# Gate, context and transposed-context transfers moved along the queue of an attention pipeline, and one group's modulation by another engine

## The chip, the cores and the metric

The program runs on one core of one Trainium2 chip. The metric is the device time of one execution in microseconds (us). Before the change it is 1631.61 us, the median of three runs (1629.51 to 1631.78). "PE" is TensorE, "DVE" VectorE, "ACT" ScalarE, "POOL" GpSimd and "SP" SyncE, which here computes nothing: it issues transfers (DMAs).

## The reference

128 sequences of 64 tokens with 128 channels pass through four layers. What matters here is the attention: 16 heads of 8 channels, in float32.

```python
# L0 (a DiT block): mod = silu(cond) @ adaln_w + adaln_b, cut in six
xm = ln(x) * (1 + sc_sa) + sh_sa
x = x + g_sa * (attend(xm @ qkv_w + qkv_b) @ sa_proj_w + sa_proj_b)      # "L0s", self
x = x + attend(ln(x) @ q_w, ctx @ kv_w) @ ca_proj_w + ca_proj_b          # "L0c", cross
x = x + g_ff * mlp(ln(x) * (1 + sc_ff) + sh_ff)
# L1: cross attention with modulated norms of x and ctx                     "L1c"
# L2: as L0, with ln(ctx) in the cross part                                 "L2s", "L2c", MLP
# L3: 1-head attention over ctx, router, three experts, a gate
```

attend is softmax(q k^T / sqrt(8)) v for each head; the sum of the weights is divided out behind the product with v.

## The kernel before

The 8192 tokens are cut into 16 groups of 8 sequences (512 tokens), which stay in SBUF as `x0` to `x15`. Two chains of attentions are run as one pipeline each: L0s and L0c over all groups (32 entries), then, behind L0's MLP, L1c, L2s and L2c (48 entries). L2's MLP and L3 follow. The order of all work is written by hand, and each engine and the queue of SP take their instructions in that order.

Each entry is worked on by two generators, `prepare` (L406) and `finish` (L555), which yield between pieces. `step(k)` (L613) is half a turn: entry `i = k // 2`, half `u = k % 2`. It issues the scores of this half (L503, then the maximum L510 and the difference L512 on DVE), exponentials of the half before (L532), weighted sums of the half before that (L545, copied by ACT into `o` at L553), and then the next pieces of the neighbours' generators through `go`. There are 80 turns, numbered here 0 to 31 (L0s, L0c) and 32 to 79.

Pieces of `prepare`, in order: load of the context `c` (cross entries alone, L414), statistics of x, normalization, transposes of the context (L440), copy of these to `cm` with, in L0c, its store to the DRAM buffer `ctxT` (L447, read again in L3), transposes of x, modulation (`modulated`: a multiplication by DVE at L353 and an addition by POOL at L354; group 0 of L0s instead by eight DVE instructions, one a sequence, L363), keys (L463, L465, L468), queries (L473, L475), values (L485, L489, L490).

Pieces of `finish`, for entry j: in the second half of turn j+1 two stores of the softmax sums from `o` to DRAM (L563), their load in another layout as `rc` (L567), four transfers that move half of `o` (L570); in the first half of turn j+2 the reciprocal by DVE (L572), its store `recs` (L574), in self attention the two loads of the gates `gt` (256 KB each, L284), and the load of `recs` broadcast over channels as `rb` (256 KB, L579); in turn j+3 the product with `rb` (POOL, L582), the bias (L584), the projection (L588) and the residual (L593, L594).

In the first half of a turn the generators are called in this order:

```python
go(prep, i); go(fin, i - 3)
if last: turned(...)
go(prep, i + 1); go(prep, i + 2); go(prep, i + 2)
go(fin, i - 2)                  # reciprocal, recs, gt, rb
if i == 0: go(prep, 3)
go(prep, i + 4); go(prep, i + 4)   # load of c; statistics
```

So all transfers of this part go through one queue, SP's: `recs` waits for the reciprocal, `rb` for the landing of `recs`, `rc` for the landing of the sums, and what stands behind one of these waits with it. Gates are loaded in turns 2 to 17 and 50 to 65, contexts in turns 12 to 27, 32 to 43 and 60 to 75, and `ctxT` is stored in turns 14 to 29. `gt` and `cm` have two buffers, `c` has three.

Of the kernel before, what the change touches and what calls it, by code (L numbers as in the profile page):

```python
# [59 lines left out]
def tile_kernel(ctx: ExitStack, tc: tile.TileContext, a: dict, out: bass.AP):  # L60
    nc = tc.nc
# [282 lines left out]
    def transposed(psum, src):  # L344

        ps = psum.tile([P, 512], F32, tag=bank_tag(), name="psT")
        for t in range(TT):
            T.transpose(ps[:, ts(t, P)], src[:, t, :], ident)  # L348
        return ps
# [56 lines left out]
    def prepare(pools, at):  # L406

        pool, psum = pools[:2]
        s, layer = at["s"], at["layer"]
        eps = 1e-5 if layer == "L1c" else 1e-6  # L410
        cross = layer[2] == "c"
        if cross:
            c = pool.tile([P, TT, P], F32, tag="c", name="c", bufs=3)
            nc.sync.dma_start(c, ctx_d[s])  # L414
        yield
        if layer == "L1c":
            mv = x_mv[:, s]
            rs = inv_std(pool, mv, eps)
        else:
            mv, rs = stats_of(pool, xs[s], eps)  # L420
        by_act = not (cross or at.get("first"))
        nb = shifts(pool, mv, rs if by_act else None, "xn")
        yield
        if by_act:
            xn = normed_by_act(pool, xs[s], nb, rs, "xn")
        else:
            xn = normed_by_pool(pool, xs[s], nb, rs, "xn", V if at.get("first") else G)
        if cross:
            cn = c
            if layer != "L0c":  # L430
                cn = pool.tile([P, TT, P], F32, tag="cn", name="cn", bufs=1)
                for t in range(TT):
                    rs, nb = (v[:, s, ctx_eps.index(eps), t : t + 1] for v in (ctx_rs, ctx_nb))
                    if s == 0:
                        G.tensor_scalar(cn[:, t, :], c[:, t, :], rs, nb, ALU.mult, ALU.add)
                    else:
                        S.activation(cn[:, t, :], c[:, t, :], AF.Identity, bias=nb, scale=rs)
        yield
        if cross:
            ps = transposed(psum, cn)  # L440
        yield
        if layer == "L1c":
            kv_in = modulated(pool, ps, "L1_xcond_Wss_kv", 0, 1, s, "cm")
        elif cross:
            kv_in = copied(pool, ps, "cm")
            if layer == "L0c":
                nc.sync.dma_start(ctxT[s], kv_in)  # L447
        yield
        ps = transposed(psum, xn)
        yield  # L450
        if layer == "L1c":
            q_in = modulated(pool, ps, "L1_xcond_Wss_q", 0, 1, s)
        elif cross:
            q_in = copied(pool, ps, "xm")
        elif at.get("first"):
            q_in = kv_in = modulated_by_batch(pool, ps, at["wmod"], 1, 0, s, by_dve=True)
        else:
            q_in = kv_in = modulated(pool, ps, at["wmod"], 1, 0, s)
        yield


        pk = psum.tile([P, 512], F32, tag=bank_tag(), name="pk")
        T.matmul(pk, at["wk"], kv_in, start=True, stop=True)  # L463
        kT = pool.tile([P, NT], F32, tag="kT", name="kT")
        S.activation(kT, pk, AF.Identity, bias=at["bk"])  # L465
        kbd = pool.tile([P, 4, NB, L], F32, tag="kbd", name="kbd")
        for j in range(4):
            (V if at.get("first") else G).tensor_scalar(  # L468
                kbd[:, j], by_batch(kT), mask[:, j : j + 1], 1.0, ALU.mult, ALU.mult
            )  # L470
        yield
        pq = psum.tile([P, 512], F32, tag=bank_tag(), name="pq")
        T.matmul(pq, at["wq"], q_in, start=True, stop=True)  # L473
        qT = pool.tile([P, NT], F32, tag="qT", name="qT")
        S.activation(qT, pq, AF.Identity, bias=at["bq"])  # L475
        at.update(qT=qT, kbd=kbd)
        yield

        vbd = vbds[turn[0] % 2]
        turn[0] += 1  # L480
        wv_pair = at["wv"].rearrange("p (i j d) -> p j i d", j=2, d=HD)
        pvv = psum.tile([P, NB, L], F32, tag=bank_tag(), name="pvv")
        for b in range(NB):
            for j in range(2):
                T.matmul(  # L485
                    pvv[ts(j, L), b, :], kv_in[:, ts(b, L)], wv_pair[:, j], start=True, stop=True
                )
        pv4 = pvv.rearrange("p b (i d) -> p b i d", d=HD)
        S.copy(vbd[0:L, :, :, 0:HD], pv4[0:L])  # L489
        S.copy(vbd[L:P, :, :, HD : 2 * HD], pv4[L:P])  # L490
        at["vbd"] = vbd
# [63 lines left out]
    def finish(pools, at):  # L555

        pool, psum = pools[:2]
        s, o = at["s"], at["o"]
        cross = at["layer"][2] == "c"

        sums = dp.tile([16, NT], F32, tag="sums", name="sums", bufs=2)
        for j in range(2):
            nc.sync.dma_start(  # L563
                sums.rearrange("(g i j) t -> j g i t", i=2, j=2)[j], o[16 + j : P : 32, :, :]
            )
        rc = pool.tile([P, L], F32, tag="rc", name="rc")
        nc.sync.dma_start(rc, sums.rearrange("h (c t) -> (h c) t", t=L))  # L567

        for g in range(4):
            nc.sync.dma_start(o[32 * g + 16 : 32 * g + 32, 0, :], o[32 * g : 32 * g + 16, 1, :])  # L570
        yield
        V.reciprocal(rc, rc)  # L572
        recs = dp.tile([16, NT], F32, tag="recs", name="recs", bufs=2)
        nc.sync.dma_start(recs.rearrange("h (c t) -> (h c) t", t=L), rc)  # L574

        if not cross:
            gt = gate_tile(pool, s, at["wp"])
        rb = pool.tile([P, NT], F32, tag="rb", name="rb")
        nc.sync.dma_start(rb, recs.unsqueeze(1).broadcast_to([16, HD, NT]))  # L579
        yield  # L580
        oT = rb
        G.tensor_tensor(oT, o[:, 0, :], rb, ALU.mult)  # L582
        bias = proj_bias[at["wp"]].unsqueeze(1).broadcast_to([P, TT, P]) if cross else gt[:, :, 1, :]
        G.tensor_tensor(xs[s], xs[s], bias, ALU.add)  # L584
        yield
        py = psum.tile([P, TT, P], F32, tag=bank_tag(), name="py")
        for t in range(TT):
            T.matmul(py[:, t, :], oT[:, ts(t, P)], w[at["wp"]][:, 0], start=True, stop=True)  # L588
        if cross:
            V.tensor_add(xs[s], xs[s], py)  # L590
        else:
            y = pool.tile([P, TT, P], F32, tag="y", name="y")
            V.tensor_tensor(y, py, gt[:, :, 0, :], ALU.mult)  # L593
            G.tensor_tensor(xs[s], xs[s], y, ALU.add)  # L594

    def attend(pools, ats):
# [5 lines left out]
        def go(gens, i):  # L602
            if 0 <= i < n:
                next(gens[i], None)
# [8 lines left out]
        def step(k, between=(), late=()):  # L613
            i, u = divmod(k, 2)
            now, last, past = (
                halves[k - d] if 0 <= k - d < 2 * n else None for d in range(3)
            )
            if now:
                now["e"] = scores(pools, now["at"], now["u"])
            for f in between:  # L620
                f()
            if last:
                last["eT"] = pools[0].tile([P, 2, 2, 512], F32, tag="eT", name="eT")
                turned(pools, last["e"], last["eT"], 0)
            if past:
                weighted(pools, past["at"], past["u"], past["eT"])
            if u == 0:
                go(prep, i)
                go(fin, i - 3)
                if last:  # L630
                    turned(pools, last["e"], last["eT"], 1)
                go(prep, i + 1)
                go(prep, i + 2)
                go(prep, i + 2)
                go(fin, i - 2)
                if i == 0:
                    go(prep, 3)
                go(prep, i + 4)
                go(prep, i + 4)
            else:  # L640
                go(fin, i - 1)
                go(prep, i + 1)
                go(fin, i - 3)
                go(prep, i + 2)
                go(prep, i + 3)
                if last:
                    turned(pools, last["e"], last["eT"], 1)
                go(prep, i + 2)
                for f in late:
                    f()  # L650
# [569 lines left out]

    def stages():
        ats = [attention_of(s, layer) for layer in ("L0s", "L0c") for s in groups]
        ats[0]["first"] = True
        ahead_1, steps_1 = attend(pools, ats)
        ahead_2, steps_2 = attend(
            pools, [attention_of(s, layer) for layer in ("L1c", "L2s", "L2c") for s in groups]
# [129 lines left out]
```

## Time and profile before

| | us |
|---|---|
| median of three runs | 1631.61 |
| the profiled execution, its own time | 1632.76 |
| its span in the trace | 1631.0 |
| PE busy | 1568.7 (96%) |
| DVE busy | 1269.3 (78%) |
| POOL busy | 1049.7 (64%) |
| ACT busy | 999.5 (61%) |
| share of the chain that ended last: PE, DVE | 83%, 11% |

The profile is of one execution. A line of the timeline gives the start and the length in us, the engine (SPq is SP's queue of issues), the line of the code, the operation, what it writes and reads, how many instructions were merged, and in brackets the idle time before with what ended it. A turn is counted here from the start of the maximum (L510) of its first half to that of the next turn. The granted TensorE clock was 0.998 over the span.

### The profile page before, as it was taken

What the parts mean: (1) busy time and instruction counts of PE and PEld (TensorE: products, weight loads), DVE (VectorE), ACT (ScalarE), POOL (GpSimd) and SP (SyncE); (2) the same over time, 40 slices, a digit from 0 to 9 for tenths busy, and PEclk for the clock granted to TensorE, in tenths of its full rate; (3) what the DMA queues carried; (4) which work ended last, traced back from release to release, by engine and by line L of the source; (5) the groups of instructions that cost most, each with busy time, mean ns of one, the idle gap of its engine ahead of it and who ended that gap; (6) DMA issues with size and microseconds to landing.
All of it is one profiled execution on the core that took longest, in us unless ns stands there. A gap on an engine that the chain in (4) does not pass through costs nothing.

```text
span 1631.0 us, 63684 instructions
## 1 busy us (share of the span) xinstructions
PE 1568.7 (96%) x27842; PEld 1099.1 (67%) x27842; DVE 1269.3 (78%) x1613; ACT 999.5 (61%) x1518; POOL 1049.7 (64%) x1680
## 2 busy tenths in 40 slices
PE   6999999999999899999999999999999999999998
PEld 4677767777554567777677677776777666666665
DVE  6999988989555699999999888987443566666666
ACT  4777766767433577777777788886334544444443
POOL 4677776766788778886677876766876333333322
PEclk9999999999999999999999999999999999999999
DMA  7333452332212022221333542221443111111100
GB/s 208 82 82 92 112 119 80 86 92 67 62 33 58 21 48 70 63 54 43 90 91 81 112 98 61 73 56 47 119 104 78 30 40 37 40 33 35 35 12 19
DMA packets 146774, 112.64 MB, mean 69 GB/s; under 512 B 36357, under 2 KB 125247, under 8 KB 146495
## 3 DMA queue, kind: packets, MB, share of 16 engines
q1 hardware_dynamic: 146288, 108.53, 26.2%
q8 instruction: 219, 3.59, 1.0%
q14 instruction: 60, 0.49, 0.1%
q10 hardware_dynamic: 207, 0.03, 0.0%
HBM read 83.99 MB, written 14.02 MB: 60 GB/s over the span
## 4 chain that ended last, share of the span: by engine, by line
PE 83%; DVE 11%; issue 2%; POOL 1%; ACT 1%; DMA 1%; SPq 0%; DVEq 0%; ACTq 0%; POOLq 0%
PE sc L503 10%; PE pp L528 9%; PE po L545 8%; PE ph L722 7%; PE ph L1111 6%; PE ph L1112 6%; PE po L1142 5%; DVE mx L510 5%; DVE e L512 5%; PE psT L348 5%; PE pq L473 4%; PE py L588 4%; PE pvv L485 4%; PE pk L463 4%; PE py L738 3%; PE py L728 3%
## 5 line engine op out<-in xcount | busy, mean ns | idle before, releaser
L532 ACT ACTIVATE eT<-pp 128x1024 f32<-128x1024 f32 x320 | 327.0, 1022 | 162.6 <-PE pp L528 160.7
L510 DVE TENSOR_REDUCE mx<-sc 128x32 f32<-128x2048 f32 x160 | 366.5, 2291 | 71.6 <-PE sc L503 71.1
L512 DVE TENSOR_TENSOR e<-sc,mx 128x2048 f32<-128x2048 f32 x160 | 366.6, 2291 | 5.4
L468 POOL TENSOR_SCALAR kbd<-kT,mask 128x512 f32<-128x512 f32 x316 | 213.4, 696 | 171.9 <-ACT kT L465 171.7
L528 PEld LDWEIGHTS pp<-ident,e 64*128 64x128 f32 x5120 | 183.8, 138 | 85.4 <-ACT eT L532 35.4
L528 PE MATMUL pp<-ident,e 64*128 64x64 f32 x5120 | 227.6, 229 | 3.9 <-DVE e L512 2.9
L503 PE MATMUL sc<-kbd,qT 32*64 32x256 f32 x5120 | 181.1, 389 | 25.2 <-DVE e L512 18.7
L723 ACT ACTIVATE h<-ph,vec 128x512 f32<-128x512 f32 x128 | 87.4, 688 | 152.3 <-PE ph L722 152.1
L545 PE MATMUL po<-eT,vbd 128*32 128x64 f32 x10240 | 177.6, 221 | 1.2 <-issue 1.2
L383 POOL TENSOR_SCALAR xn<-x,nb,rs 128x128 f32<-128x128 f32 x384 | 170.8, 460 | 5.0
L1118 ACT ACTIVATE h<-h 128x512 f32<-128x512 f32 x112 | 70.5, 630 | 148.0 <-DVE h L1114 129.0
L545 PEld LDWEIGHTS po<-eT,vbd 128*32 128x32 f32 x10240 | 151.0, 110 | 14.2 <-issue 1.9
L503 PEld LDWEIGHTS sc<-kbd,qT 32*64 32x64 f32 x5120 | 103.2, 132 | 75.3 <-DVE e L512 38.6
L336 POOL TENSOR_TENSOR rs<-rs,nhalf 128x4 f32<-128x4 f32 x128 | 130.3, 1018 | 10.7
L1114 DVE TENSOR_TENSOR h<-ph,ab 128x512 f32<-128x512 f32 x112 | 76.9, 687 | 60.8 <-PE ph L1112 60.6
L582 POOL TENSOR_TENSOR rb<-o,rb 128x512 f32<-128x512 f32 x80 | 102.4, 1280 | 29.8 <-DMA rb<-recs 18.3
L1147 DVE SCALAR_TENSOR_TENSOR acc<-po,pr,acc 128x128 f32<-128x128 f32 x192 | 67.2, 350 | 44.1 <-PE po L1142 39.6
L1111 PE MATMUL ph<-nx,w 128*128 128x512 f32 x192 | 99.9, 602 | 0.0
L1112 PE MATMUL ph<-u,w_ev 128*128 128x512 f32 x192 | 98.0, 592 | 0.0
L1142 PEld LDWEIGHTS po<-w_2o,h 128*128 128x128 f32 x768 | 92.1, 192 | 8.7 <-issue 8.4
L553 ACT COPY o<-po 128x512 f32<-128x512 f32 x160 | 93.8, 586 | 4.8 <-PE po L545 2.7
L1142 PE MATMUL po<-w_2o,h 128*128 128x128 f32 x768 | 95.8, 275 | 0.0
(260 smaller groups left out, 2810.2 us busy)
## 6 DMA issues: line engine op xcount, KB each, us to landing
rb<-recs SPq DMA_DIRECT2D x80, 256.0 KB
c<-in_ctx_dram SPq DMA_DIRECT2D x64, 256.0 KB
o<-o SPq DMA_DIRECT2D x320, 32.0 KB
gt<-gate_L_xcond_sa_proj_w SPq DMA_DIRECT2D x32, 256.0 KB
gt<-gate_L_xcond_W_proj SPq DMA_DIRECT2D x32, 256.0 KB
gt<-gate_L_xcond_W_mlp SPq DMA_DIRECT2D x32, 256.0 KB
x<-in_x_dram SPq DMA_DIRECT2D x16, 256.0 KB
ctxT<-cm SPq DMA_DIRECT2D x16, 256.0 KB
```

The costliest lines, as they stand in the source:

```text
L336: G.tensor_tensor(rs, rs, nhalf, ALU.pow)
L383: engine.tensor_scalar(xn[:, t, :], src[:, t, :], nmu[:, t : t + 1], rs[:, t : t + 1], ALU.add, ALU.mult)
L468: (V if at.get("first") else G).tensor_scalar(kbd[:, j], by_batch(kT), mask[:, j : j + 1], 1.0, ALU.mult, ALU.mult)
L503: T.matmul(sc[ts(h, L), g, ts(t2, 256)], qT[ts(g, 32), ts(b, L)], kbd[ts(g, 32), :, b, :], start=True, stop=True,)
L510: V.tensor_reduce(mx, sc.rearrange("p g (m k) -> p (g m) k", k=L), AX.X, ALU.max)
L512: V.tensor_tensor(e, sc.rearrange("p g (m k) -> p (g m) k", k=L), mx.unsqueeze(2).broadcast_to([P, 32, L]), ALU.subtract,)
L528: T.transpose(pp[:, h, ts(4 * g2 + 2 * i + t2, L)], e6[ts(h, L), 2 * gg + g2, t2, i], ident[ts(h, L), ts(h, L)],)
L532: S.activation(eT[:, gg], pp, AF.Exp, scale=HD ** -0.5)
L545: T.matmul(po[ts(g, 32), i, ts(2 * t2 + h, L)], at["vbd"][:, 4 * u + 2 * t2 + h, 2 * g + i, :], e7[:, g // 2, h, g % 2, i, t2, :], start=T ...
L1111: T.matmul(ps, wn, d["nx"], start=True, stop=False)
L1112: T.matmul(ps, we, d["u"], start=False, stop=True)
L1142: T.matmul(po[:, ex, :], d[q][:, ts(t, P)], k3["w_2o"][:, q, :], start=r == 0, stop=r == 1)
```

## The change

Four edits. The store of `ctxT` moves out of the piece that copies `cm` into the next one, which runs in the second half of the turn, behind the sums, `rc` and the moves of `o`. The loads of the gates become a piece of their own, ahead of the reciprocal's. A turn's first half calls this piece and the context's load right behind the scores, and no longer the load at its end. Group 1 of L0s is modulated by eight ACT instructions of 128x64 in place of one DVE and one POOL instruction of 128x512.

```diff
         elif cross:
             kv_in = copied(pool, ps, "cm")
-            if layer == "L0c":
-                nc.sync.dma_start(ctxT[s], kv_in)
         yield
+        if layer == "L0c":
+            nc.sync.dma_start(ctxT[s], kv_in)
         ps = transposed(psum, xn)
...
+        elif at.get("second"):
+            q_in = kv_in = modulated_by_batch(pool, ps, at["wmod"], 1, 0, s)
...
         yield
+        if not cross:
+            gt = gate_tile(pool, s, at["wp"])
+        yield
         V.reciprocal(rc, rc)
         recs = dp.tile([16, NT], F32, tag="recs", name="recs", bufs=2)
         nc.sync.dma_start(recs.rearrange("h (c t) -> (h c) t", t=L), rc)
 
-        if not cross:
-            gt = gate_tile(pool, s, at["wp"])
...
             for f in between:
                 f()
+            if u == 0:
+                go(fin, i - 2)
+                go(prep, i + 4)
             if last:
...
                 go(fin, i - 2)
                 if i == 0:
                     go(prep, 3)
-                go(prep, i + 4)
                 go(prep, i + 4)
...
-        ats[0]["first"] = True
+        ats[0]["first"] = ats[1]["second"] = True
```

`modulated_by_batch` is in the kernel already; without `by_dve` it takes its other branch:

```python
S.activation(xm[:, ts(b, L)], ps[:, ts(b, L)], AF.Identity, bias=p, scale=m)
```

In the built program DVE and POOL have one instruction less each, ACT eight more, PE's order is as before, and SP issues the same transfers in a new order: in a turn's first half [gt, gt,] c, recs, rb; in its second sums, sums, rc, four moves of o, then ctxT.

## Prediction

> **What bounds the kernel.** I read the page first, then the waits, then the timeline turn by turn.
>
> ```profile
> PE 1568.7 (96%) x27842; PEld 1099.1 (67%) x27842; DVE 1269.3 (78%) x1613; ACT 999.5 (61%) x1518; POOL 1049.7 (64%) x1680
> ...
> q8 instruction: 219, 3.59, 1.0%
> ...
> PE 83%; DVE 11%; issue 2%; POOL 1%; ACT 1%; DMA 1%; SPq 0%; DVEq 0%; ACTq 0%; POOLq 0%
> ```
>
> PE sets the time, with 62 us idle in 1631; transfers are 1% of the chain. A gain must come out of those 62 us. From the starts of L510, a turn takes 11.88 us in L0s and L2s and 11.93 to 11.96 in L0c, L1c and L2c, when nothing disturbs it. The turns above that are the place to look: turns 12 to 19 lose 5.2 us together (2.1 in turn 15, 1.35 in turn 17), turns 20 to 30 lose 4.7, turns 36, 66 and 68 lose 2.5. Turn 15 in the timeline, and the DMA share (next to last number) in two stretches of it:
>
> ```profile
> 197.63 1.32 SPq L284 DMA_DIRECT2D gt<-gate_L_xcond_sa_proj_w  x2
> 199.06 0.55 SPq L579 DMA_DIRECT2D rb<-recs  x1
> 199.65 0.59 SPq L414 DMA_DIRECT2D c<-in_ctx_dram  x1
> 200.34 1.14 SPq L563 DMA_DIRECT2D sums<-o  x2
> ...
> 203.39 1.03 PE L485 MATMUL pvv<-L_xcond_qkv_w,xm 128*64 128x64 f32 x27
> ...
> 206.31 0.34 PE L485 MATMUL pvv<-L_xcond_qkv_w,xm 128*64 128x64 f32 x5 [1.89 <-issue]
> ```
>
> ```profile
> 199.00:204.00 5.00, 4.93 (x156) 4.03 (x157) 4.23 (x3) 3.21 (x5) 3.66 (x7) 1.00 0.99 218
> 204.00:206.40 2.40, 0.51 (x18) 0.37 (x14) 2.37 (x2) 0.16 (x1) 2.39 (x3) 1.00 0.07 17
> ```
>
> PE stops between two matmuls of one loop that need nothing new. Queue 8 holds 219 packets of 16 KB for PE's instructions. In the trace's packet records they mostly start 3.5 to 6 us apart, but here one starts at 203.81, 7.6 us behind the last, just as the burst of gt, rb, c and sums (1 MB, all 16 engines busy for 5 us) drains; PE goes on 2.5 us later. The stalls that end at 232.43, 243.05, 269.93, 331.21, 356.78, 604.09, 966.50 and 991.88 stand 2.3 to 2.7 us behind such a late packet too. So **long bursts hold up PE's code**; all these stalls lie 2 to 5 us into a turn, where the bursts of L0c end. L0s's burst (gt, rb) ends at the turn's start and cost 0.3 us in ten turns.
>
> [...]
>
> **Edit 1, the start.** Gain 3.0 us.
>
> ```profile
> 17.54 1.11 PE L348 MATMUL psT<-ident,xn 128*128 128x128 f32 x4
> ...
> 22.23 0.68 DVE L353 TENSOR_TENSOR xm<-psT,mod_L_xcond_adaln_w 128x512 f32<-128x512 f32 x1
> ...
> 23.05 1.04 POOL L354 TENSOR_TENSOR xm<-xm,mod_L_xcond_adaln_w 128x512 f32<-128x512 f32 x1 [5.32 <-DVE xm L353]
> 24.15 2.07 PE L463 MATMUL pk<-xm,L_xcond_qkv_w 128*128 128x512 f32 x2 [3.59 <-POOL xm L354]
> ```
>
> The transposes end at 18.65, but DVE is at the maximum and difference until 22.3, and PE waits 3.59 us. ACT is idle from 18.51 to 20.60. No 128x64 activation is in the trace: 128x12 takes 0.21 us, 128x128 from PSUM 0.28, and four normalizations of 128x128 take 1.65 (0.41 each). I take 0.30: eight end at 18.7 + 2.4 = 21.1, pk starts at 21.15, 3.0 us earlier; from 0.21 to 0.41 the gain is 3.7 to 2.1. Behind ACT's eight stand the two value copies (20.60 becomes 21.1; PE's next use of them is at 34.9) and kT, which needs pk anyway. The next scores (26.15) may move by 3.0, since the difference they need ends at 22.31. The steps behind them are DVE and PE in turn and move along.
>
> **Edits 2 to 4, the queue.** The same bytes; what changes is what shares a burst, and what SP waits through. A quiet turn:
>
> ```profile
> 111.44 0.33 SPq L574 DMA_DIRECT2D recs<-rc  x1
> 111.81 1.31 SPq L284 DMA_DIRECT2D gt<-gate_L_xcond_sa_proj_w  x2
> ...
> 113.23 0.55 SPq L579 DMA_DIRECT2D rb<-recs  x1
> 114.48 1.16 SPq L563 DMA_DIRECT2D sums<-o  x2
> 118.22 2.29 DVE L510 TENSOR_REDUCE mx<-sc 128x32 f32<-128x2048 f32 x1 [0.17 <-PE sc L503]
> 118.63 0.32 SPq L567 DMA_DIRECT2D rc<-sums  x1
> ```
>
> Today gt's issue (1.31) is free, inside the wait for recs (1.79). Afterwards it stands before recs, and recs's data behind gt's, c's and ctxT's. SP then is a ring: rb, sums, rc, moves of o, ctxT, gt, c, recs, rb. I add up one round. rb to rc, with nothing between: 3.6 (rows without c or gt, in turns 28, 29 and 31: 3.6, 3.6, 3.7; with gt it is 5.4 above). rc with the moves: 3.4 (2.8 to 3.9 for the moves). First gt packet 1.25 behind the issue, 512 KB in 2.5; c 1.3; ctxT 1.0, first packet 0.8 behind its issue; recs 0.3; its landing to rb's issue 0.75.
> - Self alone: 7.0 + 1.25 + 2.5 + 0.3 + 0.75 = 11.8. Turn: 11.88. It just fits.
> - Gates and contexts (turns 12, 13, 60 to 65): + 1.3 = 13.1.
> - With ctxT too (14 to 17): 7.0 + 0.8 + 1.0 + 2.5 + 1.3 + 0.3 + 0.75 = 13.7.
> - Contexts and ctxT (18 to 27): 11.2. Contexts alone: less. Both fit in 11.93.
>
> A late ring is first felt by the reciprocal: rb's issue is expected 8.0 us into the turn, rc lands 5.4 later (3.6 + 1.8, from 230.96 to 232.74), and DVE comes to the reciprocal 4.5 us into the next turn. So 3.0 us of lateness are free; beyond that DVE stands, and with it mx, e and PE, since DVE's first half is full. Turns 12 to 17 run late by 2 x 1.2 + 4 x 1.8 = 9.6, less 3.0: 6.6 us lost, where 5.2 are lost now: **1.4 worse**. Turns 60 to 65: 6 x 1.2 = 7.2, less 3.0, less 2.1 which turn 62 loses anyway (POOL's cn, L435): **2.1 worse**.
>
> In return the harmful bursts go. Turns 18 to 30: today rb, c and sums (3 us) end 2 us into the turn. Afterwards ctxT and c (2.3 us) follow the moves, 3 to 6 us into the turn, where code fetched is needed later, and rb with sums is 1.7 us. Of the 4.7 us of turns 20 to 30 (stalls of 1.32, 1.29 and 0.86 among them) I take back 3.9; of the 2.5 us of L1c and L2c, 2.2. Bounds: nothing (another burst catches the code) and all 7.2. The store of ctxT waits for a copy that ACT has made half a turn before; it no longer stands before recs, where it cost up to 2 us (recs to rb 1.9 to 3.8 there). Buffers: gt's was released by L593 in the half before, c's a turn before; I see no new wait there.
>
> Sum: - 3.0 - 3.9 - 2.2 + 1.4 + 2.1 = - 5.6. Profiled execution: 1632.8 to 1627.2; that execution was 1.15 over the median, so for the median **1626.0**.
>
> **Rivals.**
> - **SP becomes the bound (slower).** The moves take 3.5 and rb to rc 3.9: a round is 0.4 longer. Ten self-only turns in a row then run 0.3 late each and use up the 3.0 us of slack, in L0 and in L2 (+ 6.0), and the twelve turns with gates and contexts lose 0.4 more each (+ 4.8): + 10.8 - 5.6 = + 5.2, so 1636.8. It decides from about 0.2 us a round. For: the largest waits in SP's view are this ring's:
>
> ```profile
> SPq L567 <- DMA sums<-o: 161.9, 85, 3.4
> SPq L574 <- DVE rc L572: 125.0, 62, 4.4
> ```
>
>  Against: SP still waits 125 us for the reciprocal, which is slack. 0.22.
> - **Only the start counts**, the bursts shift and catch other code: - 3.0, 1628.6. For: 1 MB still moves in one burst in turns 14 to 17. 0.17.
> - **SP keeps up and the stalls all go**: the rounds are shorter than summed, since a lagging ring meets an idle DMA. - 3.0 - 7.2 - 5.2 = - 15.4, 1616.2. 0.18.
> - The forecast, 1622 to 1629 by itself: 0.43.
>
> **Numbers.** A difference under 0.2% (3.3 us) can't be told from none. Range 1616.5 to 1636. Faster by more (under 1628.3): nine tenths of the forecast, the third rival, a quarter of the second: 0.61. Same: the rest of these and a few of the first: 0.20. Slower: 0.19.
>
> **What will show it.** pk of group 1 near 21 us with eight activations before it; PE's stalls on issue in turns 20 to 30 gone, and queue 8's packets there under 6 us apart; the reciprocal waiting for rc in turns 14 to 17 and 63 to 65, with turns of 13 us; rb 8 us into quiet turns. I am wrong if quiet L0s turns leave 11.88, or if PE stalls on issue stay as many.

## The result, and the profile after

The changed kernel takes 1647.84 us, the median of five runs (1647.39 to 1653.36), beside 1631.78 for the kernel before (1629.51 to 1633.59): a ratio of 1.0106, with a 95% interval of 1.0087 to 1.0125. It is 16 us slower; I had forecast 1626.0. The profiled execution took 1653.36 us and its span is 1651.6, 20.6 more than the span before. The line numbers shift by 2 ahead of the reciprocal and by 3 to 5 from it on (mx L512, e L514, sums L565, rc L569, o L572, reciprocal L577, recs L579, rb L582).

First the page: busy time of each engine, the packets of code for PE (queue 8: 219 of them for 55684 instructions of PE, one for 254), and the shares of the chain that ended last.

```profile
PE 1571.7 (95%) x27842; PEld 1102.6 (67%) x27842; DVE 1269.0 (77%) x1612; ACT 1000.8 (61%) x1526; POOL 1046.0 (63%) x1679
...
q8 instruction: 219, 3.59, 0.9%
...
PE 71%; DVE 15%; DMA 8%; issue 2%; SPq 2%; ACT 2%; POOL 1%; ACTq 0%; DVEq 0%
```

PE and DVE are busy for about as long as before (PE 3.0 us more, at a granted clock of 0.993 instead of 0.998, which is far less than the 20.6 us of the span), but PE's share of the chain falls from 83% to 71% and DMA's rises from 1% to 8%: transfers now decide when DVE and PE go on. The view of waits (us in total, times, longest) says which. For DVE and PE before, then for PE, DVE and POOL after the change:

```profile
PE sc L503 <- DVE e L512: 18.7, 31, 2.7
DVE rc L572 <- DMA rc<-sums: 7.9, 5, 3.4
```

```profile
PE sc L505 <- DVE e L514: 49.3, 60, 2.7
DVE rc L577 <- DMA rc<-sums: 44.9, 28, 3.4
POOL rb L585 <- DMA rb<-recs: 41.5, 23, 3.6
```

The same for SP, one line of the profile before and three of that after:

```profile
SPq L579 <- DMA recs<-rc: 76.1, 47, 3.3
```

```profile
SPq L582 <- DMA recs<-rc: 204.2, 79, 4.8
SPq L569 <- DMA sums<-o: 129.2, 82, 2.4
SPq L579 <- DVE rc L577: 77.9, 36, 3.6
```

The reciprocal waited 7.9 us in all for `rc` before; now 44.9. SP's wait for the landing of `recs` went from 76.1 to 204.2, and its wait for the reciprocal, which was its slack, from 125.0 to 77.9. Here is one round of SP's queue, from turn 7 into turn 8, where gates alone are loaded:

```profile
111.85 1.30 SPq L284 DMA_DIRECT2D gt<-gate_L_xcond_sa_proj_w  x2
113.19 0.60 SPq L579 DMA_DIRECT2D recs<-rc  x1
117.66 0.54 SPq L582 DMA_DIRECT2D rb<-recs  x1
118.29 1.17 SPq L565 DMA_DIRECT2D sums<-o  x2
121.20 0.32 SPq L569 DMA_DIRECT2D rc<-sums  x1
121.57 2.49 SPq L572 DMA_DIRECT2D o<-o  x4
124.17 1.29 SPq L284 DMA_DIRECT2D gt<-gate_L_xcond_sa_proj_w  x2
```

From gates to gates it is 12.32 us, and no step of it waits for an engine; a turn is 11.88. What that does to the others is seen in turn 16 (DVE, then PE):

```profile
226.77 0.55 DVE L577 RECIPROCAL rc<-rc 128x64 f32<-128x64 f32 x1 [1.86 <-DMA rc<-sums]
...
227.86 2.28 DVE L512 TENSOR_REDUCE mx<-sc 128x32 f32<-128x2048 f32 x1
230.17 2.29 DVE L514 TENSOR_TENSOR e<-sc,mx 128x2048 f32<-128x2048 f32 x1
```

```profile
232.60 1.64 PE L505 MATMUL sc<-kbd,qT 32*64 32x256 f32 x32 [1.67 <-DVE e L514]
```

DVE stands 1.86 us for `rc`, so the maximum and the difference come late, and PE stands 1.67 us for that difference. The scores buffer comes free late, and turn 16 takes 14.00 us. Where the time went, from the starts of the maximum (L510 before, L512 after; turns, us):

```
turns      before   changed   difference   (changed, second profile)
0 to 2      41.15     38.15      -3.0          38.44
3 to 11    106.99    112.17      +5.2         109.73
12 to 19   100.60    107.40      +6.8         106.51
20 to 30   135.93    133.13      -2.8         132.27
32 to 45   170.53    170.72      +0.2         169.97
46 to 59   166.57    170.89      +4.3         168.50
60 to 67    98.96    108.54      +9.6         103.48
68 to 78   132.75    132.85      +0.1         132.63
```

The last column is of a second profile of the same kernel, from the last set of experiments (e12).

The start went as forecast: the second group's modulation and the projection behind it,

```profile
18.17 2.44 ACT L365 ACTIVATE xm<-psT,mod_L_xcond_adaln_w 128x64 f32<-128x64 f32 x8
...
20.66 1.33 PE L465 MATMUL pk<-xm,L_xcond_qkv_w 128*128 128x512 f32 x2 [2.47 <-ACT xm L365]
```

eight activations in 2.44 us, 0.305 each, and `pk` at 20.66 instead of 24.15. (Of these 3.5 us, 1.15 are an earlier first maximum, 16.55 for 17.70; the profiles of the experiments have it anywhere from 16.5 to 18.2. The turns' own gain is 3.0, 2.7 in turn 0 and 0.3 in turn 1.)

### The profile page after: what moved, and what is told of

Read it like the earlier page. It is cut to its first block, busy times and chain, and to the rows that moved or that the text cites. A ratio compares the mean times of both kernels' runs of the same rounds, so it can differ in the third digit from the quotient of the medians.

```text
span 1651.6 us, 63704 instructions
## 1 busy us (share of the span) xinstructions
PE 1571.7 (95%) x27842; PEld 1102.6 (67%) x27842; DVE 1269.0 (77%) x1612; ACT 1000.8 (61%) x1526; POOL 1046.0 (63%) x1679
## 4 chain that ended last, share of the span: by engine, by line
PE 71%; DVE 15%; DMA 8%; issue 2%; SPq 2%; ACT 2%; POOL 1%; ACTq 0%; DVEq 0%
PE sc L505 8%; PE pp L530 7%; PE ph L727 7%; DVE mx L512 6%; PE ph L1116 6%; DVE e L514 6%; PE ph L1117 6%; PE po L547 6%; PE po L1147 5%; PE psT L348 4%; PE py L743 3%; DMA sums<-o 3%; PE py L733 3%; PE pq L475 3%; PE pvv L487 3%; PE pk L465 3%
## 5 line engine op out<-in xcount | busy, mean ns | idle before, releaser
L512 DVE TENSOR_REDUCE mx<-sc 128x32 f32<-128x2048 f32 x160 | 366.1, 2288 | 53.8 <-PE sc L505 53.0
L514 DVE TENSOR_TENSOR e<-sc,mx 128x2048 f32<-128x2048 f32 x160 | 366.6, 2291 | 5.4
L547 PEld LDWEIGHTS po<-eT,vbd 128*32 128x32 f32 x10240 | 152.9, 111 | 12.4 <-DVE mv L319 0.8
```

Of the source, the lines that this page charges most:

```text
L512: V.tensor_reduce(mx, sc.rearrange("p g (m k) -> p (g m) k", k=L), AX.X, ALU.max)
L514: V.tensor_tensor(e, sc.rearrange("p g (m k) -> p (g m) k", k=L), mx.unsqueeze(2).broadcast_to([P, 32, L]), ALU.subtract,)
L547: T.matmul(po[ts(g, 32), i, ts(2 * t2 + h, L)], at["vbd"][:, 4 * u + 2 * t2 + h, 2 * g + i, :], e7[:, g // 2, h, g % 2, i, t2, :], start=T ...
```

## Experiments

Theory A, formed from these views: the gates' 512 KB, now ahead of `recs` in SP's queue, make the ring (rb, sums, rc, moves of o, gates, recs, rb) longer than a turn; it falls behind a little each turn until the reciprocal waits. Theory B: the loads of the contexts at the turn's beginning, or the store of the transposed contexts, do the harm, by holding sums or PE's code. Each ratio is to the kernel before, measured beside the experiment. "Before" and "changed" name the kernel that the edit starts from. The ring, or round, is the time from the issue of one `rb` to that of the next; where nothing else is said, it is the mean of the nine rounds that end in turns 3 to 11, which hold gates and no contexts.

**e1, before with the first edit alone.**

```diff
+        elif at.get("second"):
+            q_in = kv_in = modulated_by_batch(pool, ps, at["wmod"], 1, 0, s)
...
-        ats[0]["first"] = True
+        ats[0]["first"] = ats[1]["second"] = True
```

> Before with the first edit alone: the second group's modulation as eight activations. Every theory has this step harmless: the first turn is 2.7 to 3.0 us shorter, as in the changed kernel's trace, and nothing else moves, so about 1628.7 (1627 to 1630). If it is above 1633, the ACT edit costs something later and part of the 16 us lost is its own.

1629.05 us, 0.9981 of before (0.9969 to 0.9994): 3.1 us less, 1.0 to 5.0. The first turn is 2.4 us shorter and the second 0.3. The edit is sound. Its queue is that of the kernel before, so its profile also tells how far a stage differs between executions: turns 12 to 19 take 97.33 us (100.60 before), turns 20 to 30 134.22 (135.93), turns 60 to 67 100.39 (98.96), the other stages behind the start differ by at most 1.1. This execution took 1625.30, 3.7 under the median of its kernel; the one in the profile before was 1.1 over its own.

**e2, changed with the gates back behind recs.**

```diff
-        if not cross:
-            gt = gate_tile(pool, s, at["wp"])
-        yield
         V.reciprocal(rc, rc)
         ...
         nc.sync.dma_start(recs.rearrange("h (c t) -> (h c) t", t=L), rc)
+        if not cross:
+            gt = gate_tile(pool, s, at["wp"])
```

> The changed kernel with the gate loads back in their old place, issued behind the store of recs; the three other edits stay. Theory A (the gates' 512 KB ahead of recs in SP's queue make the ring of transfers longer than a turn): recs to rb returns from 4.05 us to 2.2 in turns with gates alone, these turns return to 11.88, the issue stalls of turns 21 to 30 stay away, and the kernel takes 1622 to 1627, below the kernel before. Theory B (the context loads at the turn's start or the store behind the sums do the harm, by holding sums or PE's code): quiet L0s turns of 12.0 to 13.4 us stay and the time stays above 1640.

1620.45 us, 0.9929 (0.9912 to 0.9947): 11.6 us under the kernel before. Turns 3 to 11 are 11.88 each, turns 12 to 19 take 95.87 us (before 100.60). SP's waits:

```profile
SPq L576 <- DVE rc L574: 140.0, 68, 4.2
SPq L569 <- DMA sums<-o: 138.1, 83, 2.9
SPq L581 <- DMA recs<-rc: 96.1, 59, 4.1
```

The slack is back (140.0 for the reciprocal), the wait for `recs` is 96.1. Theory B falls: what it blames is all in this kernel, which is the fastest of the study.

**e3, before with the gates alone moved** (e2's edit the other way round, on the kernel before).

> Before with the gate loads alone moved to the turn's beginning. Theory A: L0s and L2s turns lose as in the changed kernel (recs to rb about 4 us, rounds of 12.6 to 12.8), while nothing is given back in the start and in turns 21 to 30: 1646 to 1656, slower than the changed kernel. Theory B: under 1635.

1646.7 us, 1.0085 (1.0068 to 1.0102): 13.9 us slower. `recs` to `rb` takes 3.97 us, the ring is 12.34. The gates alone are enough for the loss; they are not slower than all four edits together, as I had expected, but about the same.

**e4, changed with the gates issued by ACT at the same point of the program.**

```diff
-            nc.sync.dma_start(
+            q.dma_start(          # q = nc.scalar for the attention's gates
                 gt[ts(h, L)]
```

> The changed kernel with the gate loads issued at the same point by ACT, so that their packets are in another queue than recs and rb; bytes and moment stay. Theory A1 (order within one queue: recs' 256 B packets stand behind the 1 KB packets of the gates): recs to rb falls to 2.5 us or less, rounds fall under 11.9 and the kernel takes 1620 to 1630, unless the two issues of 0.65 us each hold ACT's exponentials up, which would show as PE waiting for eT. Theory A2 (the 16 DMA engines are full of gate data, whichever queue it comes from): recs to rb stays at 3.5 to 4 us and the time at 1642 to 1650.

1626.07 us, 0.9958 (0.9942 to 0.9973). `recs` to `rb` is 1.84 us, as expected under A1, but the trace shows that it decides less than I had meant it to: ACT does not wait through SP's ring, so its gates go out far ahead of `recs` (107.35 against 113.41) and are through before it (in the changed kernel their last packet ends 4.7 us behind the first issue, the mean of the 19 turns 3 to 11 and 50 to 59).

```profile
107.35 2.20 ACTq L284 DMA_DIRECT2D gt<-gate_L_xcond_sa_proj_w  x2
113.41 0.33 SPq L579 DMA_DIRECT2D recs<-rc  x1
115.29 0.56 SPq L582 DMA_DIRECT2D rb<-recs  x1
```

It also has a loss of its own: the first gate load holds ACT up in turn 2, so that an exponential waits 6.2 us and turns 0 to 2 end 4.9 us later than in the changed kernel.

**e5 and e6, before with one edit each:** the context load at the turn's beginning; the store of transposed contexts one yield later.

```diff
+            if u == 0:                      # e5
+                go(prep, i + 4)
             if last:
...
-                go(prep, i + 4)
                 go(prep, i + 4)
```

```diff
-            if layer == "L0c":              # e6
-                nc.sync.dma_start(ctxT[s], kv_in)
         yield
+        if layer == "L0c":
+            nc.sync.dma_start(ctxT[s], kv_in)
```

> Before with the context loads alone moved to the turn's beginning. The changed kernel with the gates back took 1620.5 where the start alone gives 1629.1, so the two other edits together are worth some 8.5 us. If the context load is what gave it (it leaves the burst of rb, c and sums and sums no longer wait behind it): 1622 to 1626, with the stalls of turns 15, 17, 25 and 27 shorter. If it is the store: about 1630.6, as before.

> Before with the store of the transposed contexts alone moved behind the moves of o. If the store ahead of recs is what costs: 1622 to 1626, with recs to rb down from 2.4 to 2.6 us to 2.2 in turns 14 to 27. If the context load is: about 1630.6. If the two must go together (each burst alone still drains when code is wanted): 1627 to 1631 here and in the run with the context loads alone.

e5: 1626.1 us, 0.9978 (0.9968 to 0.9988). e6: 1624.39 us, 0.9968 (0.9957 to 0.9979). Each gives something, 3.6 and 5.2 us; neither expectation that puts all of it on one edit holds, nor the one that they work only together. The sum of the three single edits is 11.9, and e2, which has all three, gives 11.6: these three add. What they have in common shows in PE's stalls on issue in turns 12 to 30 (times, us; gaps over 0.15 us) and in the packets of PE's code that start over 6 us behind the one before, out of some 45:

```
           stalls    us    late packets
before        7      6.3       11
e1            4      3.7       11
e5            2      1.6        6
e6            4      1.8        6
e2            2      0.6        3
changed       2      1.4        8
```

**e8, the three other edits, the gates issued by ACT where the reciprocal stands.**

```diff
         nc.sync.dma_start(recs.rearrange("h (c t) -> (h c) t", t=L), rc)
+        if not cross:
+            gt = gate_tile(pool, s, at["wp"], nc.scalar)
```

> The three other edits stay, and the gates are issued by ACT, not early but where the reciprocal stands in the program, so that their packets and recs's are under way together, in two queues. In the earlier run with ACT's queue they went out 5 us ahead of recs and were through before it, so that run did not tell order from load. Theory A1 (order within one queue): recs to rb stays under 2.6 us though the gates are in flight, 1619 to 1626. Theory A2 (the 16 DMA engines are full, whichever queue): recs to rb 3.5 to 4 us, rounds over 12.3, 1638 to 1650.

1624.35 us, 0.9968 (0.9956 to 0.9979). This run does what e4 didn't: gates and `recs` are issued within a microsecond of each other.

```profile
109.28 0.58 ACTq L284 DMA_DIRECT2D gt<-gate_L_xcond_sa_proj_w  x1
109.80 0.33 SPq L576 DMA_DIRECT2D recs<-rc  x1
109.90 0.63 ACTq L284 DMA_DIRECT2D gt<-gate_L_xcond_sa_proj_w  x1
113.31 0.56 SPq L581 DMA_DIRECT2D rb<-recs  x1
```

`recs` to `rb` is 3.19 us in turns 3 to 11 and 3.41 in turns 50 to 59, between what A1 (under 2.6) and A2 (3.5 to 4) expected; the time is A1's, since the ring still fits (11.91). The packet records say why. The last 256 B packet of `recs` ends, in the mean of these 19 turns, 2.4 us behind its issue; in the changed kernel, where it stands behind the gates in one queue, 3.3; alone (the kernel before, where the gates' data come behind it) 1.3. So of the 2.0 us that `recs` loses, about 1.1 come with the gates under way in another queue, and 0.9 more with the gates ahead of it in its own; the split is rough, since the gates are issued 1.7 us ahead of `recs` in the changed kernel and 0.5 us here.

**e9, half of the gates ahead of recs, half behind it.**

```diff
-            gt = gate_tile(pool, s, at["wp"])
+            gt = gate_tile(pool, s, at["wp"], None, (0,))
         yield
         ...
         nc.sync.dma_start(recs.rearrange("h (c t) -> (h c) t", t=L), rc)
+        if not cross:
+            gate_tile(pool, s, at["wp"], gt, (1,))
```

> The changed kernel with half of the gates (256 KB) ahead of recs and the other half behind it. Theory A with a threshold (the loss begins where a round exceeds the turn of 11.88): recs to rb about 2.8 us, rounds of 11.4 plus what SP waits, so self-only turns fit again and only turns with gates and contexts lose a little: 1621 to 1628, that is nearly all of the loss gone for half of the bytes. A loss in proportion to the bytes ahead of recs would give 1634.

1626.13 us, 0.9976 (0.9964 to 0.9989). Turns 3 to 11 take 106.97 us, turns 46 to 59 166.41: as quiet as before. Only turns 12 to 19, with contexts too, lose (101.68; e2 95.87). Against e2, half of the bytes cost some 8 us (0.9976 / 0.9929), the whole 22 to 29 (1.0064 and 1.0106 / 0.9929, from e12 below and the first runs); in the turns with gates alone half of them cost nothing, where the whole cost 2.7 to 5.2 us in turns 3 to 11. So in these turns the loss is not in proportion to the bytes; a threshold at the length of the turn, as theory A has it, fits.

**e10, changed without the moves of o in the queue** (the second half of the heads' sums is left out of the result).

```diff
-        for g in range(4):
-            nc.sync.dma_start(o[32 * g + 16 : 32 * g + 32, 0, :], o[32 * g : 32 * g + 16, 1, :])
```

> The changed kernel without the four moves of o in SP's queue, so the second half of the heads' sums is left out of the result; gates, contexts and their places stay. Ring theory: a round loses 2.4 us, 12.6 becomes 10.2, and gates and contexts 13.3 become 10.9, so SP is never late although recs still stands behind the gates: recs to rb stays near 4 us, L0s and L2s turns are 11.88, 1612 to 1622. If the gates' place harms in another way (PE's code packets held, or POOL waiting for rb): above 1640.

1621.59 us, 0.9943 (0.9931 to 0.9955): the loss is gone although the gates are still ahead of `recs`. The time held at the upper end of 1612 to 1622; "recs to rb stays near 4 us" did not: it is 1.9. SP's waits, first lines:

```profile
SPq L577 <- DVE rc L575: 357.1, 80, 6.6
...
SPq L580 <- DMA recs<-rc: 123.0, 80, 3.2
```

SP now waits for the reciprocal in all 80 rounds, and in that wait the gates, issued 5.6 us ahead of `recs`, are through. This is a point that I had missed: the gates stand in the way of `recs` only when the ring is late already, and then they make it later.

**e7, the three other edits, the gates issued behind rb.**

```diff
         nc.sync.dma_start(rb, recs.unsqueeze(1).broadcast_to([16, HD, NT]))
+        if not cross:
+            gt = gate_tile(pool, s, at["wp"])
```

> The three other edits, with the gates issued behind rb instead of between recs and rb. The ring theory can be tried on a place not yet seen: recs to rb 1.8 us (recs alone), then the sums stand behind the gates' issue (1.31) and their data (in the changed kernel: first packet 1.66 behind the issue, 3.1 us of data), so rb to rc 0.6 + 1.66 + 3.1 + 1.5 = 6.9 instead of 3.6; with 3.3 for the moves a round is 12.0. That is at the turn's 11.88: 1620 to 1630, little or nothing lost against the kernel with the gates between. If what harms is only that recs stands behind the gates, it is 1616 to 1620, below that kernel.

1639.18 us, 1.0056 (1.0039 to 1.0074): slower, outside my 1620 to 1630. The terms were about right (`recs` to `rb` 2.1 where I had 1.8, `rb` to `rc` 6.1 where I had 6.9), and so was the ring: 12.2, and 11.9 in turns 50 to 59, where I had 12.0; but I had summed only rounds with gates alone. With contexts behind the gates it is 13.9 in the rounds that start in turns 14 to 17 and 13.6 in those from turns 60 to 65, and those turns take 13.4 and 13.0 us, with the reciprocal waiting in turns 14 to 18. Turns 3 to 11 take 2.7 us more than in e2, but not by the ring: the reciprocal waits in none of them, and PE stands on issue for 1.4 us in turn 5 and 1.3 in turn 10. Nothing stands between `recs` and `rb` here, so it is not only that wait which counts, but the whole round.

**e11 and e12, changed with the context loads back in their old place** (e5's edit undone), and changed once more as it is.

> The changed kernel with the context loads back in their old place, behind rb; gates early, store behind the moves, start by ACT. The parts don't add: the gates alone cost 14 us, the other three edits alone give 11, all four cost 17. Ring theory: in turns 12 to 17 and 60 to 67 the early context load adds 0.8 to 1.3 us to rounds that the gates had already made too long; without it the store and the start keep what they gave, and the time is 1636 to 1642. If the contexts' place doesn't matter once the gates are early: 1645 to 1649.

> The changed kernel once more, unchanged, beside these on one chip, for a second profile: its first one was that of its longest execution. All theories: a ratio of 1.009 to 1.013; the turns with gates and contexts (12 to 17, 60 to 67) lose in the same places, and turns 3 to 11 lose between 2 and 5 us, with rounds of 12.4 to 12.7.

e11: 1640.65 us, 1.0057 (1.0045 to 1.0069). e12: 1640.59 us, 1.0064 (1.0051 to 1.0076). e11 is where I expected it by the ring, but so is e12, which I had expected above it: with the gates early, the contexts' place makes no difference that can be measured, the second reading. And e12's loss, 10.6 us, is smaller than that of the first set of runs (16.1), with intervals that don't touch. The two profiles lose in the same turns (table above) by different amounts: in the 19 turns with gates alone the gates' data take 3.08 us in the first and 2.93 in the second. The sign and place are shown; the size depends on a few tenths of a microsecond a round, and I can't say what sets these from one set of runs to the other.

## Why the prediction was wrong

**Step that failed: the sum "7.0 + 1.25 + 2.5 + 0.3 + 0.75 = 11.8. Turn: 11.88. It just fits."** Measured in the rounds that end in turns 3 to 11 and 50 to 59 of the first profile, and, for the gates, in the same turns of the profile before, which I had in hand:

```
                              forecast   measured   before
rb to rc, rc with the moves      7.0        6.6
gates' issue to first packet     1.25       1.66      1.49
gates' data, 512 KB              2.5        3.08      3.08
recs behind them                 0.3        0.25
landing to rb's issue            0.75       0.80
sum                             11.8       12.4
```

The two terms of the gates were too small by 1.0, the rest too large by 0.4. The new place of the gates is not what made them longer: in the profile before, the shortest of the 19 turns has 1.43 and 2.56 us, so both of my values lay below every row of it, and with its means the sum would have been 12.6. In 12 of the 19 turns one of PE's 16 KB code packets lies in the gates' burst; their data then take 3.27 us, without it 2.76. The whole round in the trace, with what SP waits besides, is 12.39 in turns 3 to 11 and 12.63 in turns 50 to 59 (12.23 and 12.40 in the second profile). So the rival "SP becomes the bound" took place: it asked for a round longer by 0.2 to decide, and it is longer than the forecast 11.8 by 0.6 and 0.8 (0.4 and 0.6). But it is so by the gates' terms; the moves and `rb` to `rc`, which the rival named, were shorter than in the sum. I had priced it at 0.4 (1636.8) and given it 0.22. A sum of five terms, each known to some tenths, that ends 0.08 from its limit is no forecast that it fits; it was at best an even chance.

**A second gap: the slack is spent before the context turns.** I gave the 3.0 us of slack to turns 12 to 17 and again to turns 60 to 65. The turns with gates alone ahead of each had spent it: in turns 50 to 53 `rb` goes out 9.0, 10.4, 11.1 and 12.0 us into the turn and the reciprocal waits from turn 53 on; in L0s it stands at 12.1 in turn 2 already. The rounds with contexts are longer than forecast, too: those with gates and contexts (13.1 forecast) 13.8 where they end in turns 12 to 14 and 14.0 in turns 60 to 65, those with the store (13.7) 14.1 where they end in turns 15 to 17 (in the second profile 13.0, 13.4 and 14.4). So turns 12 to 19 lost 6.8 us more than before (5.9 in the second profile) where I had 1.4, and turns 60 to 67 9.6 (4.5) where I had 2.1. Turns 3 to 11 and 46 to 59, for which I had nothing, lost 5.2 and 4.3 (2.7 and 1.9).

**A third: whether `recs` stands behind the gates depends on the ring.** A ring that is early issues the gates 5.6 us ahead of `recs` and passes them in SP's wait for the reciprocal (e10: 1.9 us from `recs` to `rb`). A late one issues `recs` directly behind them (4.05 us). "A lagging ring meets an idle DMA", from my third rival, is the reverse of what happens here.

**Right: edit 1.** 3.0 us forecast, 3.0 in the trace, 2.7 in the trace of e1 and 3.1 (1.0 to 5.0) in its time; 0.30 us for an activation, 0.305 measured.

**Right in its direction, its size open: the code stalls.** I took back 3.9 of the 4.7 us that turns 20 to 30 lost; they are shorter by 2.8 and 3.7 us in the two profiles, and without the gates' move (e2) by 3.2. Against the profile of e1, with the old queue, it is only 1.1, 2.0 and 1.5. The times of e1, e5, e6 and e2 show that both edits behind it pay, 8.5 us together (0.9929 / 0.9981 of 1631). In L1c and L2c, where I took back 2.2, nothing came: turns 32 to 45 and 68 to 78 are within 0.6 us of before in both profiles. The late packets and the stalls go down together (11 to 3, 6.3 us to 0.6), which supports bursts as the cause; the runs do not show that nothing else moved the stalls, which also differ from execution to execution: e1's profile has 3.7 us of them with 11 late packets, as many as before.

**Why the parts don't add.** The gates cost 13.9 us alone and 1.0064 / 0.9929, some 22 us, on top of the other edits. In turns 12 to 19 e2 takes 4.7 us less than the profile before (1.5 less than e1's); with the gates early these turns take 106 to 107 us with or without the other edits (e3 106.02), and PE stands on issue nowhere in them, in e3 as little as in the changed kernel. I read this so: the ring sets these turns, and what PE would wait for its code lies inside the ring's waits. There the gain is covered rather than lost; no run tests it apart.

**My signs.** `pk` near 21 with eight activations: seen. Stalls of turns 20 to 30 gone: mostly (1.4 us of stalls are left; late packets there 6 before, 1 after). The reciprocal waiting in turns 14 to 17 and 63 to 65: seen, and in self-only turns too. `rb` 8 us into quiet turns: 12.4. Quiet L0s turns that leave 11.88, the sign against me: 13.00, 13.41 and 13.02 in turns 3, 7 and 11.

## What to carry to other kernels

Where one queue holds a chain of dependent small transfers that comes round once a turn, sum the round with every transfer in it and compare it with the turn before anything is put ahead of a small store in that chain. Take each term as the mean over all its rows, not from the quickest. A sum as near to the turn as this one (11.8 to 11.88; 12.39 and 12.63 measured) means that the ring may become the bound, and then every late turn adds up (`rb` at 9.0, 10.4, 11.1 and 12.0 us in turns 50 to 53). In this kernel the large load, which nothing waits for soon, belonged behind the small store, in a wait that the queue has anyway (between `recs` and `rb`: 1.3 us of issue, with 2.2 us from `recs` to `rb` before and 1.84 in e4, where no issue stands between), and not at the earliest point of the same queue. Undo the parts of a change one by one: here three of four edits together made the kernel 11.6 us faster, and the fourth hid it.

## What the runs showed of the hardware

The last of the 128 packets of 256 B of a store ended 1.3 us behind its issue alone (before), 2.4 with 512 KB under way in another engine's queue (e8), and 3.3 behind the same 512 KB in its own (changed), each the mean of 19 turns. In turn 7 of e8 the last packet of `recs` ends at 2.37 us, while the gates' packets go on to 3.41; in one queue (changed, the mean of the 19 turns) it ends 0.25 us behind the last of them. In e8 the first packet of `recs`, too, starts only 1.63 us behind its issue in that turn, 0.83 alone (before, the mean of 19 turns); another queue was half a remedy.

The same two loads of the gates took 2.76 us where no 16 KB code packet fell into them and 3.27 where one did; in the profile before it is 2.78 and 3.26, in the second profile of the changed kernel 2.59 and 3.06. The code packet itself takes about 1.1 us there. Why the loads take longer then is not shown: the trace names the queue of a packet, and not its DMA engine. In a ring with 0.1 us to spare (11.8 of 11.88 in the forecast's sum), half a microsecond is the difference between slack and bound.

The packets of queue 8 go with PE's instructions: between the starts of two lie 255 of these in the mean where the packets start up to 12 us apart, and 246 where it is 13 to 39 us (before).
